# Expert slots of 256 rows, and half slots of 128 for an expert's remaining rows, in a conv-attention hybrid with a mixture of experts

## The chip, the core and the metric

The kernel runs on one core of one Trainium2 chip. The metric is the device time of one execution in microseconds (us); the time before is the median of three runs. The profile is one more execution, taken by the hardware profiler.

## What is computed

The input is an image of 256 channels and 64 x 64 places. A first layer does windowed linear attention on the normalized image and adds it. A second layer takes the 4096 places as tokens of 256 channels, adds a softmax attention of 8 heads, and then a mixture of experts, which is the part that the change touches:

```python
logits = xt @ Wr + br                       # 8 experts
top_p, top_idx = jax.lax.top_k(softmax(logits), 2)
weights = top_p / top_p.sum(axis=-1, keepdims=True)
xe = layernorm(xt) * ln_g + ln_b            # gain and shift of each expert
h = gelu(xe @ W1 + b1)                      # 256 -> 1024
y = h @ W2 + b2                             # 1024 -> 256
out = sum over the two chosen experts of weights * y
```

All of it is in f32. The reference works out every expert for every token; the kernel works out only the 2 x 4096 = 8192 pairs of token and chosen expert.

## The kernel before

The stages run one after the other: convolution and windowed attention, softmax attention, routing, expert slots, ending. The change touches routing and expert slots.

**Routing** (lines 1190 to 1365). The tokens' normalized rows z are made on ScalarE (L1224) in a buffer of their own and written to `zrows` in DRAM on SP's queue (L1228). VectorE finds each token's two experts and counts the rows of each expert (`upto`, L1271). A slot is 256 rows of one expert. Each expert gets as many slots as its rows fill, rounded up (`more`, `slots`, `ends`, L1276 to L1287). From `ends` come the expert of each slot (`past`, `owner`, `expert_of`, L1289 to L1297), a flag whether more than 36 slots are needed (`more_slots`, L1298), and the first row of each expert (`begins`). The place of each pair (`row`, then `at`, `pos`) is turned around by one-hot matmuls (L1334 to L1340: `line` and `piece` are built on VectorE and ScalarE for 8 token tiles at a time, and 64 bf16 matmuls add into one PSUM bank): for each row of each slot, the token to read (`source`) and the place to write (`target`). Rows that hold no token read token 0 and write to spare rows of `yrows`.

**Slots** (`run`, L1367 to L1432). The usual program has 36 slots; 3 more stand in a branch behind them, taken if `more_slots` is set (L1437 on). For each slot `weights` (L1170 to L1183) reads the slot's expert number into a register of SP and loads, on SP's queue and in this order, `cols` (first bias, gain and shift, L1179), `w1` (1 MB, L1180), `w2` (1 MB, L1181) and `b2` (L1182), each into one of two buffers. `load` also gathers two tiles of 128 rows from `zrows` with indirect DMAs on GpSimd (L1377; four buffers). `enter` transposes them on TensorE (L1391, four transposes) and applies gain and shift on VectorE (L1395). Then, for 8 hidden tiles, two matmuls add into a PSUM buffer `hp` of 256 columns (L1416; two buffers in turn), and ScalarE's Gelu empties it (L1417). After the first layer, `enter` of the next slot comes, and then the second layer: for each of the two row tiles 8 matmuls of 256 columns into `yp` (L1423), the bias added on VectorE (L1425), and an indirect DMA that scatters 128 rows to `yrows` (L1427). The framework's scheduler orders each engine's instructions by these dependences; so transposes and gathers can stand elsewhere than in the source.

**Ending** (L1442 on). Both experts' rows are read back, weighted, added to the tokens, transposed and written out.

Of the kernel before, what the change touches and what calls it, by code (L numbers as in the profile page):

```python
# [30 lines left out]
P = 128  # L31
# [15 lines left out]
NE = 8  # L47
HID = 1024
SLOT = 256
NS = (2 * N + NE * (SLOT - 1)) // SLOT  # L50
USUAL = 2 * N // SLOT + NE // 2
TAME = 60.0
# [8 lines left out]
    "k": {"sums": NCH // 4 * NW * D, "spread": NCH // 4 * NW * P, "before8": CH, "sides": NB * (SW + IMG + 1)},  # L61
    "m": {"rank": NE, "iota": P, "before": P, "ones": P, "number": 1, "high": 2 * NT, "spare": NS * SLOT // P},
}
# [7 lines left out]
def constants():  # L71
# [34 lines left out]
    out[:, _AT["high"]] = np.arange(2 * NT)[None, :]  # L106
    out[:, _AT["spare"]] = 1 + 2 * N + p[:, None] + P * np.arange(NS * SLOT // P)[None, :]
    return out
# [3 lines left out]
def tile_conv_attn_hybrid(ctx: ExitStack, tc: tile.TileContext, a: dict, out: bass.AP):  # L112
# [27 lines left out]
    def tok(i):  # L140
        return slice(P * i, P * (i + 1))
# [996 lines left out]


    with ExitStack() as phase:  # L1140
        pool = lambda name, bufs: phase.enter_context(tc.tile_pool(name=name, bufs=bufs))
# [6 lines left out]
        zrows = dram.tile([N, C], F32, name="zrows")  # L1148
        yrows = dram.tile([2 * N + NS * SLOT, C], F32, name="yrows")

# [11 lines left out]

        source = small.tile([P, NS * SLOT // P], mybir.dt.int32, name="source")
        target = small.tile([P, NS * SLOT // P], mybir.dt.int32, name="target")
        expert_of = small.tile([P, NS], mybir.dt.int32, name="expert_of")
        more_slots = small.tile([P, 1], mybir.dt.int32, name="more_slots")
# [3 lines left out]
        def weights(work, s):  # L1170

            e = nc.values_load(
                expert_of[:1, s : s + 1], engines=(mybir.EngineType.SP,), min_val=0, max_val=NE - 1
            )
            w1 = work.tile([P, KC, HID], F32, name="w1")
            w2 = work.tile([P, NH, C], F32, name="w2")
            b2 = work.tile([P, C], F32, name="b2")
            cols = work.tile([P, NH + 2 * KC], F32, name="cols")
            nc.sync.dma_start(cols, crows[bass.ds(e, 1)].rearrange("o p n -> p (o n)"))  # L1179
            nc.sync.dma_start(w1, a["L1_ffn_W1"][bass.ds(e, 1)].rearrange("o (k p) h -> p (o k) h", p=P))  # L1180
            nc.sync.dma_start(w2, a["L1_ffn_W2"][bass.ds(e, 1)].rearrange("o (k p) d -> p (o k) d", p=P))  # L1181
            nc.sync.dma_start(b2, a["L1_ffn_b2"][bass.ds(e, 1)].rearrange("o d -> (o d)").partition_broadcast(P))  # L1182
            return w1, w2, b2, cols  # L1183
# [6 lines left out]
        with ExitStack() as routing:  # L1190
            pool = lambda name, bufs: routing.enter_context(tc.tile_pool(name=name, bufs=bufs))
            r_ps = routing.enter_context(psum("r_ps", 2))
            bank, _ = banks(r_ps)
            big = pool("r_big", 1)
            r_work = pool("r_work", 2)
# [25 lines left out]
            nc.vector.scalar_tensor_tensor(less, norm.mean, -1.0, again, op0=ALU.mult, op1=ALU.mult)  # L1221
            z = big.tile([P, NT, C], F32, name="z")
            for i in range(NT):
# [21 lines left out]
            for n in range(2):  # L1245
# [26 lines left out]


            iota = cst["iota"]
            steps = small.tile([P, N // SLOT], F32, name="steps")
            nc.vector.tensor_scalar_mul(steps, iota[:, : N // SLOT], float(SLOT))  # L1276
            more = small.tile([P, NE, N // SLOT], F32, name="more")
            nc.vector.tensor_tensor(
                more,
                upto[:, :, NT - 1].unsqueeze(2).to_broadcast([P, NE, N // SLOT]),  # L1280
                steps.unsqueeze(1).to_broadcast([P, NE, N // SLOT]),
                ALU.is_gt,
            )
            slots = small.tile([P, NE], F32, name="slots")
            nc.vector.tensor_reduce(slots, more, AX.X, ALU.add)
            ends = small.tile([P, NE], F32, name="ends")
            nc.vector.tensor_tensor_scan(ends, on[:, 0, 1 : NE + 1], slots, 0.0, op0=ALU.mult, op1=ALU.add)  # L1287
            past = small.tile([P, NS, NE], F32, name="past")
            nc.vector.tensor_tensor(  # L1289
                past,  # L1290
                iota[:, :NS].unsqueeze(2).to_broadcast([P, NS, NE]),
                ends.unsqueeze(1).to_broadcast([P, NS, NE]),
                ALU.is_ge,
            )
            owner = small.tile([P, NS], F32, name="owner")
            nc.vector.tensor_reduce(owner, past, AX.X, ALU.add)
            nc.vector.tensor_scalar_min(expert_of, owner, NE - 1.0)  # L1297
            nc.vector.tensor_single_scalar(more_slots, ends[:, NE - 1 :], float(USUAL), op=ALU.is_gt)  # L1298
            begins = small.tile([P, NE], F32, name="begins")
            nc.vector.tensor_sub(begins, ends, slots)  # L1300
            nc.vector.tensor_scalar_mul(begins, begins, float(SLOT))

            row = small.tile([P, NE, NT], F32, name="row")
            nc.vector.tensor_sub(row, upto, per_tile)
            nc.vector.tensor_add(flat(row), counts[:, : NE * NT], flat(row))
            nc.vector.tensor_add(row, row, begins.unsqueeze(2).to_broadcast([P, NE, NT]))

# [3 lines left out]

            NPC = NS * SLOT // P
            G = 8
# [3 lines left out]
            for n in range(2):  # L1317
# [13 lines left out]
                for i8 in range(0, NT, G):  # L1331
                    some = lambda v, n: v[:, i8 : i8 + G].unsqueeze(1).to_broadcast([P, n, G])
                    line = r_work.tile([P, P, G], BF16, name="line")
                    nc.vector.tensor_tensor(line, some(within, P), counter, ALU.is_equal)  # L1334
                    piece = r_work.tile([P, 3, NPC, G], BF16, name="piece")
# [3 lines left out]
                    for i in range(G):  # L1339
                        nc.tensor.matmul(  # L1340
                            back[:, : 2 * NPC].rearrange("p (m n) -> p m n", m=2),
                            line[:, :, i],
                            piece[:, 1:, :, i],
                            start=n == 0 and i8 + i == 0,
                            stop=n == 1 and i8 + i == NT - 1,
                        )

            for n in range(2):
# [18 lines left out]
        def run(slots, work, ps):  # L1367


            def load(s):  # L1370

                of = weights(work, s)
                xs = []
                for j in range(SLOT // P):
                    xs.append(work.tile([P, C], F32, name="xs", bufs=4))
                    q = SLOT // P * s + j
                    nc.gpsimd.indirect_dma_start(  # L1377
                        out=xs[j],
                        out_offset=None,
                        in_=zrows[:, :],  # L1380
                        in_offset=bass.IndirectOffsetOnAxis(ap=source[:, q : q + 1], axis=0),
                    )
                return *of, xs

            def enter(slot):

                *_, cols, xs = slot
                tp = ps.tile([P, KC, SLOT], F32, tag="tp", name="ps_tp")
                for j in range(SLOT // P):
                    for k in range(KC):  # L1390
                        nc.tensor.transpose(tp[:, k, tok(j)], xs[j][:, tok(k)], ident)  # L1391
                xe = work.tile([P, KC, SLOT], F32, name="xe")
                for k in range(KC):
                    gain, shift = (slice(NH + KC * n + k, NH + KC * n + k + 1) for n in range(2))
                    nc.vector.tensor_scalar(  # L1395
                        xe[:, k, :],
                        tp[:, k, :],
                        cols[:, gain],
# [7 lines left out]
            xe = enter(ahead)  # L1406
            for s in slots:
                slot, x_now = ahead, xe
                if s + 1 in slots:
                    ahead = load(s + 1)  # L1410
                w1, w2, b2, cols, _ = slot
                hid = work.tile([P, NH, SLOT], F32, name="hid")
                for n in range(NH):
                    hp = ps.tile([P, SLOT], F32, tag="hp", name="ps_hp")
                    for k in range(KC):
                        nc.tensor.matmul(hp, w1[:, k, tok(n)], x_now[:, k, :], start=k == 0, stop=k == KC - 1)  # L1416
                    nc.scalar.activation(hid[:, n, :], hp, AF.Gelu, bias=cols[:, n : n + 1])  # L1417
                if s + 1 in slots:
                    xe = enter(ahead)
                for j in range(SLOT // P):  # L1420
                    yp = ps.tile([P, C], F32, tag="yp", name="ps_yp")
                    for n in range(NH):
                        nc.tensor.matmul(yp, hid[:, n, tok(j)], w2[:, n, :], start=n == 0, stop=n == NH - 1)  # L1423
                    y = work.tile([P, C], F32, name="y", bufs=4)
                    nc.vector.tensor_add(y, yp, b2)  # L1425
                    q = SLOT // P * s + j
                    nc.gpsimd.indirect_dma_start(  # L1427
# [5 lines left out]

        run(range(USUAL), slot_work, experts.enter_context(psum("m_ps", 2)))
        experts.close()
        more_slots = nc.values_load(more_slots[:1, :1], min_val=0, max_val=1)  # L1436
        with (  # L1437
# [3 lines left out]
        ):  # L1441
            run(range(USUAL, NS), work, ps)  # L1442

# [58 lines left out]
```

## Time and profile before

| what | us |
|---|---|
| median of 3 runs (2933.38 to 2937.23) | 2935.82 |
| the profiled execution | 2937.02 |
| its span, first to last instruction | 2935.2 |

| stretch, us from the span's start | stage | length | PE busy | DVE busy | ACT busy | GB/s |
|---|---|---|---|---|---|---|
| 0 to 1060 | convolution, windowed attention | 1060.0 | 989.25 | 760.88 | 334.86 | |
| 1060 to 2310 | softmax attention | 1250.0 | 1240.48 | 1192.27 | 1022.79 | 5 |
| 2310 to 2374 | routing | 64.0 | 32.21 | 38.82 | 27.39 | 153 |
| 2374 to 2889.5 | 36 expert slots | 515.5 | 515.29 | 65.18 | 136.36 | 183 |
| 2889.5 to 2935.2 | ending | 45.7 | 17.45 | 26.04 | 11.57 | 279 |

How to read it: PE is TensorE's matmuls, PEld its weight loads, DVE is VectorE, ACT is ScalarE, POOL is GpSimd, SP issues DMAs. In a timeline line stand the start, the length, the engine, the line of the kernel, the operation, tile written <- tiles read, the shapes and how many were merged, and in brackets the idle time before and what ended it. In a line of groups stand, behind the count, the busy time in us and the mean in ns of one, then the idle time before. A TensorE operation in f32 shows as two records for each matmul and one for each transpose, each with its own weight load.

### The profile page before, as it was taken

The numbers are of one execution on the slowest core, as the hardware profiler recorded it, in microseconds if no ns is written. First come the engines' busy times: TensorE is split into PE (matmuls) and PEld (weight loads), VectorE is DVE, ScalarE is ACT, GpSimd is POOL, SyncE is SP. The second block draws the span as 40 slices with busy tenths as digits, with TensorE's granted clock in tenths as the row PEclk, the third lists the DMA queues.
The fourth block names the chain that finished last, engine by engine and source line by source line (L and its number), as shares of the span: only waits on it lengthen the run. The fifth ranks groups of instructions, "written<-read, shape, count | busy, mean of one in ns | idle before, by whom it ended". The sixth has DMA issues, their size and how long they took to land. (4 is left out here: it accounts for less than half of the span.)

```text
span 2935.2 us, 63107 instructions
## 1 busy us (share of the span) xinstructions
PE 2794.7 (95%) x26358; PEld 1352.3 (46%) x26358; DVE 2083.2 (71%) x3005; ACT 1533.0 (52%) x2134; POOL 720.3 (25%) x816
## 2 busy tenths in 40 slices
PE   6899999989999989999999999999999699999996
PEld 5466442735644354222222222222222268888884
DVE  5776768577677877999999999999999821111113
ACT  3242323124233213888888888888888622222222
POOL 1085858119485621000000000000000022222220
PEclk9999999999999999999999999999999879999997
DMA  5000000000000000000000000000000155555555
GB/s 142 6 3 3 2 3 2 7 1 3 4 2 3 1 19 1 5 5 5 5 5 5 5 5 5 5 5 5 5 5 5 53 182 200 191 189 195 192 196 198
DMA packets 97930, 137.35 MB, mean 47 GB/s; under 512 B 18242, under 2 KB 79272, under 8 KB 97636
## 3 DMA queue, kind: packets, MB, share of 16 engines
q1 hardware_dynamic: 82360, 105.31, 10.9%
q0 software_dynamic: 6912, 18.88, 2.2%
q10 hardware_dynamic: 8364, 9.02, 0.9%
q8 instruction: 210, 3.44, 0.5%
q14 instruction: 84, 0.69, 0.1%
HBM read 115.07 MB, written 18.12 MB: 45 GB/s over the span
## 5 line engine op out<-in xcount | busy, mean ns | idle before, releaser
L1001 ACT ACTIVATE pe<-ps_two 128x1024 f32<-128x1024 f32 x1024 | 993.1, 1022 | 150.0 <-PE ps_two L991 145.4
L1008 DVE TENSOR_TENSOR total<-total,pe 128x1024 f32<-128x1024 f32 x928 | 1058.2, 1217 | 0.0
L991 PE MATMUL ps_two<-qk 32*128 32x512 f32 x4096 | 629.1, 639 | 3.6 <-POOLq L946 1.9
L959 PE MATMUL ps_acc<-pe,v 128*32 128x512 f32 x4096 | 546.4, 605 | 0.1
L554 ACT COPY sm<-ps_sc 128x384 f32<-128x384 f32 (+4 forms) x486 | 232.4, 512 | 459.5 <-PE ps_sc L678 276.4
L558 POOL TENSOR_TENSOR sm<-sm,mask 128x192 f32<-128x192 f32 (+3 forms) x460 | 380.2, 861 | 231.6 <-ACT sm L554 231.0
L991 PEld LDWEIGHTS ps_two<-qk 32*128 32x128 f32 x4096 | 204.8, 183 | 418.7 <-PE ps_two L991 222.2
L558 DVE TENSOR_TENSOR sm<-ps_sc,mask 128x384 f32<-128x384 f32 (+3 forms) x708 | 324.2, 518 | 91.7 <-PE ps_sc L678 90.2
L1417 ACT ACTIVATE hid<-ps_hp,cols 128x256 f32<-128x256 f32 x288 | 136.4, 473 | 382.8 <-PE ps_hp L1416 382.0
L1266 POOL MEMSET on<- 128x256 f32 x1 | 0.3, 311 | 1175.1 <-PE ps_den L959 1175.1
L959 PEld LDWEIGHTS ps_acc<-pe,v 128*32 128x32 f32 x4096 | 80.7, 108 | 389.4 <-issue 376.2
L1416 PE MATMUL ps_hp<-xe,w 128*128 128x256 f32 x1152 | 257.0, 381 | 0.0
L1423 PE MATMUL ps_yp<-w,hid 128*128 128x256 f32 x1152 | 254.6, 379 | 0.0
L678 PE MATMUL ps_sc<-qk 32*128 32x192 f32 (+3 forms) x2688 | 245.3, 446 | 5.2 <-DVE sm L558 2.9
L1423 PEld LDWEIGHTS ps_yp<-w,hid 128*128 128x128 f32 x1152 | 216.4, 190 | 28.1
L1416 PEld LDWEIGHTS ps_hp<-xe,w 128*128 128x128 f32 x1152 | 208.5, 190 | 42.1 <-ACT hid L1417 5.0
L694 PE MATMUL ps_acc<-sm,v 128*32 128x192 f32 (+3 forms) x2688 | 216.6, 423 | 0.8 <-POOL sm L558 0.8
L1395 DVE TENSOR_SCALAR xe<-ps_tp,cols 128x256 f32<-128x256 f32 x72 | 35.9, 540 | 248.8 <-PE ps_tp L1391 228.7
L558 POOL TENSOR_TENSOR sm<-sm,ycut 128x384 f32<-128x384 f32 (+4 forms) x150 | 150.7, 1025 | 140.4 <-ACT sm L554 140.2
L678 PEld LDWEIGHTS ps_sc<-qk 32*128 32x128 f32 x2688 | 126.4, 186 | 124.0 <-DVE sm L558 70.4
L1425 DVE TENSOR_TENSOR y<-ps_yp,b 128x256 f32<-128x256 f32 x72 | 30.6, 425 | 208.1 <-PE ps_yp L1423 208.1
L558 DVE TENSOR_TENSOR sm<-ps_sc,ycut 128x512 f32<-128x512 f32 (+4 forms) x250 | 127.7, 562 | 64.8 <-PE ps_sc L609 62.7
(231 smaller groups left out, 2252.5 us busy)
## 6 DMA issues: line engine op xcount, KB each, us to landing
w<-in_L_ffn_W SPq DMA_DIRECT2D x72, 1024.0 KB
b<-in_L_ffn_b SPq DMA_DIRECT2D x36, 128.0 KB
rows<-in_x SPq DMA_DIRECT2D x16, 256.0 KB
zrows<-z SPq DMA_DIRECT2D x4, 1024.0 KB
y<-yrows SPq DMA_DIRECT2D x8, 512.0 KB
y<-yrows ACTq DMA_DIRECT2D x8, 512.0 KB
rec<-recs SPq DMA_DIRECT2D x60, 64.0 KB
x<-in_x ACTq DMA_DIRECT2D x4, 512.0 KB
```

The source lines that it names most:

```text
L554: nc.scalar.copy(sm[:, :used], sc[:, :used])
L558: engine.tensor_mul(to, of, mk.unsqueeze(1).to_broadcast(list(to.shape)))
L678: nc.tensor.matmul(scs[h][:, at : at + n], kT[hs[h], tok(i)], qT[hs[h], CH * ix + CELL * c0 : CH * ix + CELL * c1], start=True, stop=True, ...
L694: nc.tensor.matmul(acc[hs[h], CELL * c0 : CELL * c1], v[:, i, hs[h]], sms[h][:, at : at + n], start=not begun[0], stop=last and at == plac ...
L959: nc.tensor.matmul(to[D * hd : D * (hd + 1), :], lhsT(hd), rhs[:, hd, :], start=start, stop=stop, skip_group_check=True,)
L991: nc.tensor.matmul(sc[hd // 2][:, hd % 2, :], qk[hs, 1, g, tok(i)], qk[hs, 0, g, chunk(qc)], start=True, stop=True,)
L1001: nc.scalar.activation(pe[:, pair, :], s, AF.Exp, scale=C**-0.5)
L1008: add = nc.vector.tensor_add(to, first[:, pair, :] if i == 1 else to, pe[:, pair, :])
L1395: nc.vector.tensor_scalar(xe[:, k, :], tp[:, k, :], cols[:, gain], cols[:, shift], op0=ALU.mult, op1=ALU.add,)
L1416: nc.tensor.matmul(hp, w1[:, k, tok(n)], x_now[:, k, :], start=k == 0, stop=k == KC - 1)
L1417: nc.scalar.activation(hid[:, n, :], hp, AF.Gelu, bias=cols[:, n : n + 1])
L1423: nc.tensor.matmul(yp, hid[:, n, tok(j)], w2[:, n, :], start=n == 0, stop=n == NH - 1)
```

## The change

A row block of 128 becomes the unit. An expert gets one whole slot of 256 rows for each 256 of its rows, and one more if over 128 are left; if 1 to 128 are left, it gets a half slot of 128 rows. The whole slots stand first (32 of them, 64 units), the half slots behind (up to 8). The usual program has 32 whole slots and 4 half ones, a half one after whole slots 4, 12, 20 and 28 (counted from 0); 4 more units of 128 rows, each with its own load of weights, stand in the branch. `more_slots` is set if more than 68 units are needed.

In a half slot the first layer's matmuls and Gelus have 128 columns instead of 256, and the second layer has one row tile. The weights are loaded whole for each slot as before. `w1` and `w2` get three buffers each, `cols` and `b2` keep two. z is put into the attention's activation buffer `act`. `begins` has a second half for the half slots, and `row` gets it where a row lies behind its expert's whole slots (`rest`, `inside`). The experts of the slots (`owners`) are worked out later, after the second `line` of the one-hot matmuls. The one-hot pieces get 72 instead of 78 columns.

```diff
-NS = (2 * N + NE * (SLOT - 1)) // SLOT
-USUAL = 2 * N // SLOT + NE // 2
+NS = 2 * N // SLOT
+NU = 2 * NS + NE
+USUAL = 2 * NS + NE // 2
...
-            w1 = work.tile([P, KC, HID], F32, name="w1")
-            w2 = work.tile([P, NH, C], F32, name="w2")
+            w1 = work.tile([P, KC, HID], F32, name="w1", bufs=3)
+            w2 = work.tile([P, NH, C], F32, name="w2", bufs=3)
...
-            z = big.tile([P, NT, C], F32, name="z")
+            z = act.rearrange("p k n -> p (k n)").rearrange("p (i c) -> p i c", c=C)
...
-            nc.vector.tensor_scalar_mul(steps, iota[:, : N // SLOT], float(SLOT))
+            nc.vector.tensor_scalar(
+                steps, iota[:, : N // SLOT], float(SLOT), float(P), op0=ALU.mult, op1=ALU.add
+            )
...
+            size = small.tile([P, 2, NE], F32, name="size")
+            nc.vector.tensor_reduce(size[:, 0], more, AX.X, ALU.add)
+            inside = small.tile([P, NE], F32, name="inside")
+            nc.vector.tensor_scalar_mul(inside, size[:, 0], float(SLOT))
+            nc.vector.tensor_tensor(size[:, 1], total, inside, ALU.is_gt)
+            nc.vector.tensor_scalar_mul(size[:, 0], size[:, 0], 2.0)
...
+            def owners():
...
+                nc.vector.tensor_reduce(owner, past, AX.X, ALU.add)
+                nc.vector.tensor_copy(expert_of, owner)
+                nc.vector.tensor_single_scalar(expert_of, expert_of, NE - 1, op=ALU.bitwise_and)
+                nc.vector.tensor_single_scalar(more_slots, ends[:, 1, NE - 1 :], float(USUAL), op=ALU.is_gt)
...
-            nc.vector.tensor_add(row, row, begins.unsqueeze(2).to_broadcast([P, NE, NT]))
+            by_tile = lambda v: v.unsqueeze(2).to_broadcast([P, NE, NT])
+            rest = small.tile([P, NE, NT], F32, name="rest")
+            nc.vector.tensor_tensor(rest, row, by_tile(inside), ALU.is_ge)
+            nc.vector.tensor_mul(rest, rest, by_tile(begins[:, 1]))
+            nc.vector.tensor_add(row, row, by_tile(begins[:, 0]))
+            nc.vector.tensor_add(row, row, rest)
...
+                    if n == 0 and i8 == G:
+                        with tc.issue_after(made.ins):
+                            owners()
...
-                        nc.tensor.matmul(hp, w1[:, k, tok(n)], x_now[:, k, :], start=k == 0, stop=k == KC - 1)
-                    nc.scalar.activation(hid[:, n, :], hp, AF.Gelu, bias=cols[:, n : n + 1])
+                        nc.tensor.matmul(
+                            hp[:, :n], w1[:, k, tok(m)], x_now[:, k, :n], start=k == 0, stop=k == KC - 1
+                        )
+                    nc.scalar.activation(hid[:, m, :n], hp[:, :n], AF.Gelu, bias=cols[:, m : m + 1])
...
-        run(range(USUAL), slot_work, experts.enter_context(psum("m_ps", 2)))
+        usual = []
+        for s in range(NS):
+            usual.append((2 * s, 2 * s + 1))
+            if s % (2 * NS // NE) == NS // NE:
+                usual.append((2 * NS + s // (2 * NS // NE),))
+        assert len(usual) == NS + USUAL - 2 * NS
+        run(usual, slot_work, experts.enter_context(psum("m_ps", 2)))
...
-            run(range(USUAL, NS), work, ps)
+            run([(q,) for q in range(USUAL, NU)], work, ps)
```

## The prediction

> **What bounds the kernel now.** I read the page first (busy shares by slice), then busy time by stage, then the timeline of one slot, then the groups split by shape, for durations of the shapes that the change makes more of.
>
> Page, the slices, and two groups:
>
> ```profile
> PE   6899999989999989999999999999999699999996
> PEclk9999999999999999999999999999999879999997
> L1416 PE MATMUL ps_hp<-xe,w 128*128 128x256 f32 x1152 | 257.0, 381 | 0.0
> L1423 PE MATMUL ps_yp<-w,hid 128*128 128x256 f32 x1152 | 254.6, 379 | 0.0
> ```
>
> The expert slots are the last stretch of 9s, with the clock granted nearly in full. Between 2374.0 and 2889.5 us TensorE is busy 515.29 of 515.50 us: it sets the time there, and 36 slots run in it (1152 records over 32 a slot). One slot on the timeline:
>
> ```profile
> 2618.44 7.09 PE L1416 MATMUL ps_hp<-xe,w 128*128 128x256 f32 x32
> 2619.55 0.47 ACT L1417 ACTIVATE hid<-ps_hp,cols 128x256 f32<-128x256 f32 x1 [7.79 <-PE ps_hp L1416]
> 2620.08 5.05 PEld L1416 LDWEIGHTS ps_hp<-xe,w 128*128 128x128 f32 x24 [0.15 <-ACT hid L1417]
> ...
> 2625.36 0.60 PE L1391 MATMUL ps_tp<-cst,xs 128*128 128x128 f32 x4
> ...
> 2625.80 7.07 PE L1423 MATMUL ps_yp<-w,hid 128*128 128x256 f32 x32
> ...
> 2632.71 0.59 PE L1416 MATMUL ps_hp<-xe,w 128*128 128x256 f32 x2
> ```
>
> From start to start: first layer 2625.36 - 2618.44 = 6.92 us (32 records, 0.216 each), four transposes 0.44 (0.11 each), second layer 6.91, in all 14.27 us. A matmul in f32 is two records. ScalarE is idle 0.39 to 0.41 us between Gelus, so it follows TensorE. The line at 2620.08 is the one to keep: the third group of a slot reuses the first group's PSUM buffer (there are two), and its weight load starts 0.06 after that Gelu ends (2619.55 + 0.47). Here this is just in time.
>
> **What the change does to the slots.** The eight experts' row counts, worked out by the reference on its own inputs, are 1063, 1010, 1041, 992, 1033, 995, 1042, 1016. Before: 5+4+5+4+5+4+5+4 = 36 slots, all in the usual program. After: the remainders over 1024 are 39, 17, 9 and 18, so four half slots, and the others still fill four whole ones: 32 whole and 4 half, 68 units, exactly the usual program. The extra branch stays untaken (68 is not above 68). So four slots of 14.27 us become half slots.
>
> Cost of a half slot on TensorE. The second layer has one row tile of 8 matmuls instead of two: 16 records x 0.216 = 3.46. It has two transposes: 0.22. The first layer keeps its 16 matmuls and their weight loads, with 128 moving columns instead of 256: 32 records. Two things can keep these from costing half.
>
> First the weight load that goes with each record. The nearest row is an f32 matmul of 128 columns with its own 128x128 weights in the convolution stage:
>
> ```profile
> 591.83 0.30 PEld L436 LDWEIGHTS ps_two<-cstk,kt 128*128 128x128 f32 x2
> 591.89 0.43 PE L436 MATMUL ps_two<-cstk,kt 128*128 128x128 f32 x2
> 592.05 0.30 PEld L440 LDWEIGHTS ps_two<-cstk,kt 128*128 128x128 f32 x2
> 592.16 0.34 PE L440 MATMUL ps_two<-cstk,kt 128*128 128x73 f32 x2
> 592.27 0.19 PEld L355 LDWEIGHTS ps_two<-act,w 128*128 128x128 f32 x1
> ```
>
> Loads start 0.22 apart for two, so 0.11 each, while the matmuls run; the transposes above (each with its own load) also take 0.11. The Trainium skill, "TensorE: Matmul & The Clock Gate", section "The mechanism", speaks against the change: weight loads overlap a running matmul only where the row groups differ; its section "LDWEIGHTS (loading the stationary operand)" gives a load as columns over 1.2, 107 ns for 128. By that rule a record would be 0.107 + 0.107 = 0.214, the first layer would cost as much as a whole one (6.85), a half slot 0.22 + 6.85 + 3.46 = 10.53, and the change only 4 x 3.74 = 15.0 us. By the rows the load hides and the record is 0.11 (at worst 0.135, the 0.27 from L436's start to L440's over two): first layer 3.52 (4.32). I take the rows; L1416's own 0.216 leaves no room for a load in series either, as twice 0.11 is all it has.
>
> Second, ScalarE. A group of two matmuls lasts 4 x 0.11 = 0.44 and its Gelu of 128 columns is not in the trace. Bounds from the copies of the same engine out of PSUM:
>
> ```profile
> L554 ACT COPY sm<-ps_sc 128x384 f32<-128x384 f32 x250 | 110.5, 482 | 187.3 <-PE ps_sc L678 146.8 <-PE ps_sc L609 32.6 <-POOL sm L558 7.6
> L554 ACT COPY sm<-ps_sc 128x256 f32<-128x256 f32 x24 | 8.2, 374 | 24.2 <-PE ps_sc L609 24.2
> ```
>
> (482 - 374)/128 = 0.84 ns a column, so 473 - 108 = 365 ns; the floor is half of 473, 237. With two PSUM buffers, groups go in pairs. Pair begins at 0: first group's last record starts at 0.33, lasts about 0.27 (L1391's mean is 290), Gelu starts some 0.06 later, 0.66, ends at 1.03; weight load 0.06 later, matmul 0.11 after that: 1.20. The pair needs 0.88 of TensorE, so it waits. The built order puts the next slot's four transposes one after each pair, which fills 0.11 of each gap. First layer with these four transposes: 3 x 1.20 + 0.88 + 0.11 = 4.59 instead of 3.52 + 0.44 = 3.96. Half slot, without the next slot's transposes: 0.22 + 4.15 + 3.46 = 7.83 (bounds: 7.20 if the wait is all covered, 8.2 with a Gelu of still 473 ns, whose pair takes 1.31). Each saves 14.27 - 7.83 = 6.44, four 25.8 us.
>
> **What else moves in the slots.** Weights are still loaded whole, 36 times, so four loads come 7.8 us after the one before instead of 14.3. The windows show the ceiling:
>
> ```profile
> 2500.00:2700.00 200.00, 200.00 (x955) 171.41 (x954) 25.83 (x56) 53.02 (x112) 55.00 (x56) 1.00 0.59 194
> 2615.00:2617.00 2.00, 2.00 (x11) 1.77 (x10) 0.42 (x1) 0.00 (x0) 1.00 (x1) 1.00 1.02 418
> ```
>
> Last two columns: DMA share and GB/s. The mean is 194, the burst while one weight matrix comes in 418. In the built order SP's queue takes, for slot s+1, cols (waits for the last Gelu of slot s-1), w1 and w2 (with a third buffer no wait beyond that), b2 (waits for the last y of slot s-1; the loads of s+2 are queued behind it). The slot after a half one thus has its weights issued after the first layer of the slot before the half: 6.91 + 7.83 = 14.7 us ahead, against about 2.1 MB: the three windows of 2 us from 2619 (120, 371 and 173 GB/s, one matrix and the gathers) carried 1.3 MB in 6 us, so 10 us. Hidden; the third buffer is what lets w2 go out with w1, since before it was issued only after the slot's last matmul (2618.63). The gathers (L1377), one for a half slot as its one scatter, stand one to two slots ahead of their transposes in POOL's order and y and xs keep four buffers: no wait that I can find; price 0, and a few us if one is late.
>
> **Routing, before the first slot (2310 to 2374).** On VectorE from "more" (2337.84) to "at" (2340.70) there are 2.86 us now. The four operations on the slots' owners leave this path (0.48, 0.47, 0.18 and 0.15 busy, but overlapping: some 0.9 from start to start); three more of 128x256 (0.42 busy, about 0.41 apart) and four more of at most 16 columns (0.16 busy, about 0.17 apart) come in, 1.9. Net +1.0. The owners' past and reduce over 640 elements (0.48 for 312, so about 0.8 each) with four small ones, some 2.2 us, fall in VectorE's wait of 2.84 us before 2349.20; if that cover were gone, up to 2.2. The expert numbers come 9 us later, about 2349.5; SP's queue has the weight loads behind them, w1 goes out near 2352 instead of 2343, and the first L1416 starts at 2373.85, so 20 us hide it; what they no longer collide with is the zrows writes. z in act's place waits for the last L940, ended 2321.6, while z starts at 2330. The one-hot matmuls, 64 of 156 columns at 0.283 in series, get 144: between nothing and 64 x 0.022 = 1.4 gained; I take 0.7, as no row separates load from stream there. Net +0.3 (from -0.4 to +3).
>
> **Sum.** -25.8 + 0.3 = -25.5 us. The profiled execution took 2937.02 (span 2935.2), 1.2 above the median of 2935.82, so 2911.5 for it and 2910.3 for the median.
>
> **Rivals.**
> - Half is half: Gelu and handshakes fit under a pair's matmuls and transpose (0.99). For it: ScalarE is idle 0.39 of each 0.87. Against: 1.20, and still 1.07 with a Gelu of 237. Half slot 7.20: -28.3 + 0.3, 2907.8.
> - Weight loads in series, the skill's rule: -15.0 + 0.3, 2921.1. Against: L436 and L1391.
> - A load or gather is late at each half slot, up to 3 us: 2911 to 2922. Against: 14.7 us of lead.
> - Loads cannot go above their mean of 194 GB/s: 36 loads then take the time of 36 slots, no gain, 2936. Against: 418.
> - The slower side: the branch is taken. Place: after the usual slots. If routing on the chip gave 69 units or more, four half slots follow, each with its own load of 2.1 MB: about 10 for the first load and gather, then 4 x 8 with nothing else to hide behind, +42: 2935.8 - 25.5 + 42 = 2952. It decides at one unit, for which some expert must cross a multiple of 128 upwards: the nearest is 1016, 9 rows short. In the reference's scores only 4 tokens have second and third expert within 0.001. So 3 in 100.
>
> **Chances.** Likeliest case 0.66 (2908 to 2914), half is half 0.14, series 0.06, late transfers 0.08, no gain 0.03, branch 0.03. The range 2905 to 2918 takes in the first two and the better part of late transfers. About 0.2% (6 us) is what a measurement of this kernel can tell: faster by more 0.94, within it 0.03, slower 0.03.
>
> **What would show it.** In the profile after: L1416's counterpart in two shapes, 1024 records of 256 columns and 128 of 128; L1417 256 of 256 columns and 32 of 128 at 365 ns; a half slot of 7.8 us, the weight loads of its pairs waiting for ACT, three waits of 0.2 to 0.3 each. A half slot near 10.5 with no ACT wait is the series rival; a pause at the start of L1416 or L1423 of the slot after a half one is the late load; L1416 in a second program past the usual slots is the branch. I am wrong if whole slots are no longer 14.27.

## The result, and the profile after

| | before | after |
|---|---|---|
| median, us (5 runs each) | 2935.91 | 2909.11 |
| lowest to highest | 2933.38 to 2937.83 | 2907.35 to 2911.62 |
| profiled execution, us | 2937.02 | 2911.62 |
| its span | 2935.2 | 2909.8 |

The ratio is 0.9907, 95% interval 0.9893 to 0.992: 26.8 us less, where 25.5 were forecast. The two profiled executions differ by 25.4. Runs of one kernel differ by up to 4.5, so the medians alone cannot tell the 26.8 from the 25.5; the stretches of the traces below are finer.

On the page of the changed kernel the slots' slices look as they did, nine tenths busy at a clock granted nearly in full (a slice is a fortieth of the span, so counting slices does not show the saving):

```profile
PE   6899999989999988999999999999999969999996
PEclk9999999999999999999999999999999969999997
```

The groups split by shape, in the stretch of the slots (count, busy us, mean ns, idle before):

```profile
L1453 PE MATMUL ps_hp<-xe,w 128*128 128x256 f32 x1024 | 228.5, 381 | 0.0
...
L1456 ACT ACTIVATE hid<-ps_hp,cols 128x256 f32<-128x256 f32 x256 | 121.4, 474 | 326.3 <-PE ps_hp L1453 326.3
...
L1453 PE MATMUL ps_hp<-xe,w 128*128 128x128 f32 x128 | 18.1, 284 | 0.0
...
L1456 ACT ACTIVATE hid<-ps_hp,cols 128x128 f32<-128x128 f32 x32 | 11.8, 368 | 34.1 <-PE ps_hp L1453 33.0
```

There are 1024 first-layer records of 256 columns and 128 of 128, so 32 whole and 4 half slots, and none behind them: the branch was not taken. A Gelu of 128 columns takes 368 ns. The first half slot on the timeline:

```profile
2448.05 1.05 PE L1453 MATMUL ps_hp<-xe,w 128*128 128x128 f32 x8
...
2448.74 0.77 ACT L1456 ACTIVATE hid<-ps_hp,cols 128x128 f32<-128x128 f32 x2 [7.15 <-PE ps_hp L1453]
...
2448.94 0.27 PE L1428 MATMUL ps_tp<-cst,xs 128*128 128x128 f32 x1
2449.16 0.97 PEld L1453 LDWEIGHTS ps_hp<-xe,w 128*128 128x128 f32 x8 [0.19 <-ACT hid L1456]
2449.16 1.16 PE L1453 MATMUL ps_hp<-xe,w 128*128 128x128 f32 x8
...
2450.33 1.16 PE L1453 MATMUL ps_hp<-xe,w 128*128 128x128 f32 x8
...
2451.50 1.16 PE L1453 MATMUL ps_hp<-xe,w 128*128 128x128 f32 x8
...
2452.60 3.62 PE L1462 MATMUL ps_yp<-w,hid 128*128 128x256 f32 x16
```

Eight records are a pair of groups; inside a pair the records start 0.111 to 0.112 apart. After the first pair comes one transpose of the next slot, and the next pair's weight load waits for the Gelu. The second to fourth pair start 1.17 us apart (2449.16, 2450.33, 2451.50), the first 1.11 before the second, though each holds only 0.89 of matmuls and 0.11 of transpose. From start to start the half slot lasts 8.01 us with the next slot's four transposes in it, and so do the other three; the slot before it, with two transposes instead of four, lasts 14.05. A half slot's own share is thus 8.01 - 0.22 = 7.79, and it saves 14.27 - 7.79 = 6.48.

Where the time went, by starts of instructions in the two traces. `chosen` (the sum of the two one-hot choices on VectorE, at 2333.80 before and 2335.68 after) stands ahead of everything that the change alters but z's buffer; the 1.88 us between the two is within the spread of earlier stages (2332.96 to 2337.86 in all the profiles here).

| stretch | before | after | difference |
|---|---|---|---|
| chosen to first first-layer matmul | 40.05 | 39.56 | -0.49 |
| first slot's start to last slot's start | 501.44 | 475.51 | -25.93 |
| last slot's start to the end | 59.95 | 59.09 | -0.86 |

The second row is four times 6.48 (25.92); the first slot is 0.31 shorter, and one whole slot took 14.55, as its first Gelu came 0.28 later than in other slots and TensorE waited for it (why it came later stays open). The third row is within the spread of the ending: another profile of the kernel before, with z changed only (below), has 59.20. The sum is -27.28; with the 1.88 by which the changed kernel came later to `chosen` it is the profiles' -25.4.

### The profile page after: what moved, and what is told of

Its sections match the earlier page's. It is cut to its first block, busy times and chain, and to the rows that moved or that the text cites. A ratio compares the mean times of both kernels' runs of the same rounds, so it can differ in the third digit from the quotient of the medians.

```text
span 2909.8 us, 62928 instructions
## 1 busy us (share of the span) xinstructions
PE 2769.2 (95%) x26286; PEld 1329.9 (46%) x26286; DVE 2082.3 (72%) x3009; ACT 1529.6 (53%) x2134; POOL 712.4 (24%) x808
## 5 line engine op out<-in xcount | busy, mean ns | idle before, releaser
L1456 ACT ACTIVATE hid<-ps_hp,cols 128x256 f32<-128x256 f32 (+1 forms) x288 | 133.1, 462 | 360.4 <-PE ps_hp L1453 359.3
L1453 PE MATMUL ps_hp<-xe,w 128*128 128x256 f32 (+1 forms) x1152 | 246.6, 370 | 0.0
L1462 PE MATMUL ps_yp<-w,hid 128*128 128x256 f32 x1088 | 240.8, 379 | 0.0
L1453 PEld LDWEIGHTS ps_hp<-xe,w 128*128 128x128 f32 x1152 | 201.1, 190 | 39.7 <-ACT hid L1456 5.6
L1462 PEld LDWEIGHTS ps_yp<-w,hid 128*128 128x128 f32 x1088 | 204.2, 190 | 26.4
L1432 DVE TENSOR_SCALAR xe<-ps_tp,cols 128x256 f32<-128x256 f32 (+1 forms) x72 | 34.8, 525 | 239.3 <-PE ps_tp L1428 217.5
L561 POOL TENSOR_TENSOR sm<-sm,ycut 128x384 f32<-128x384 f32 (+4 forms) x150 | 150.8, 1024 | 140.9 <-ACT sm L557 140.6
```

The costliest lines, as they stand in the source:

```text
L561: engine.tensor_mul(to, of, mk.unsqueeze(1).to_broadcast(list(to.shape)))
L1432: nc.vector.tensor_scalar(xe[:, k, :n], tp[:, k, :n], cols[:, gain], cols[:, shift], op0=ALU.mult, op1=ALU.add,)
L1453: nc.tensor.matmul(hp[:, :n], w1[:, k, tok(m)], x_now[:, k, :n], start=k == 0, stop=k == KC - 1)
L1456: nc.scalar.activation(hid[:, m, :n], hp[:, :n], AF.Gelu, bias=cols[:, m : m + 1])
L1462: nc.tensor.matmul(yp, hid[:, m, tok(j)], w2[:, m, :], start=m == 0, stop=m == NH - 1)
```

## Experiments

The ratios below are against runs of the kernel before on the same chip.

**Four PSUM buffers for the first layer.**

```diff
-                    hp = ps.tile([P, SLOT], F32, tag="hp", name="ps_hp")
+                    hp = ps.tile([P, SLOT], F32, tag="hp", name="ps_hp", bufs=4)
```

> The changed kernel with four instead of two PSUM buffers for the first layer's groups (hp). Theory (a half slot costs 0.6 us more than half because its groups of 0.44 us go in pairs that wait 1.17 us for the Gelu of 0.37 and its handshakes): with four buffers the wait goes, the half slot with the next slot's transposes falls from 8.01 to about 7.4 us, four half slots save 2.4 us, and whole slots stay at 14.27. Rival (the weight loads, 0.11 each at best, set the pace in the half slot too): 8.01 stays, no change. Rival (ScalarE's own Gelus are the bound, 0.37 each): 8 x 0.40 = 3.2 us are less than the matmuls' 3.5, so no.

Measured: 2906.40 us, ratio 0.9892 (0.9875 to 0.9908); its interval overlaps the change's, so what follows rests on the trace. Its half slots take 7.46 us, its whole ones 14.25. The timeline of its first half slot:

```profile
2446.13 3.73 PE L1453 MATMUL ps_hp<-xe,w 128*128 128x128 f32 x32
...
2446.82 3.44 ACT L1456 ACTIVATE hid<-ps_hp,cols 128x128 f32<-128x128 f32 x8 [7.15 <-PE ps_hp L1453]
...
2449.70 0.60 PE L1428 MATMUL ps_tp<-cst,xs 128*128 128x128 f32 x4
...
2450.14 3.62 PE L1462 MATMUL ps_yp<-w,hid 128*128 128x256 f32 x16
```

All 32 records run through in 3.57 us, 0.112 each, each with its own weight load; the wait for the Gelu is gone (between 2440 and 2850 us the weight loads of the first layer wait 5.0 us for Gelus in the changed kernel, and in this one such a wait is no longer listed). So the 0.55 us by which a half slot was longer than its matmuls was that wait, and the loads do not set the pace. The saving of four half slots is 2.2 us; from the first slot's start to the last one's it is 3.9, mainly as the first slot also falls, from 16.85 to 15.01.

**Two buffers for w1 and w2.**

```diff
-            w1 = work.tile([P, KC, HID], F32, name="w1", bufs=3)
-            w2 = work.tile([P, NH, C], F32, name="w2", bufs=3)
+            w1 = work.tile([P, KC, HID], F32, name="w1")
+            w2 = work.tile([P, NH, C], F32, name="w2")
```

> The changed kernel with two buffers for w1 and w2 as before, instead of three. Theory (the loads have 14 us or more ahead of their use with either count; the third buffer is not what hides them): slots stay at 14.27 and 8.01 us, time within 1 us of the changed kernel's. Rival (the prediction's sentence that the third buffer is what lets w2 go out with w1, and that this hides the load behind a short slot): the slot after a half one starts its second layer late, some 1 to 3 us at each of four places, 4 to 12 us slower than the changed kernel.

Measured: 2911.16 us, ratio 0.9906 (0.989 to 0.9923). Slots of 14.27 and 8.01 as in the changed kernel, from first to last 475.34 us against 475.51. With two buffers the second weight matrix for the slot behind the first half slot is issued 6.05 us after the first (2443.66 and 2449.71), with three 0.61 after it (2442.20 and 2442.81), and no matmul waits for a weight in either. The third buffer brings nothing here: the rival, which is the prediction's own sentence, falls. In the routing it even seems to cost: from `chosen` to the first slot it is 38.88 us with two buffers and 39.56 with three, most of it before the first gather (see the end).

**The owners in their old place.** `owners()` is called ahead of `row`, and no longer inside the one-hot loop.

> The changed kernel with the slots' owners worked out where they were before, ahead of row, instead of in VectorE's wait during the one-hot matmuls. Theory (before the change ScalarE's z held up the first one-hot piece by 1.0 us, the change's longer chain on VectorE used this up and both now arrive together): the four owner operations, about 2.2 us, now come on the path; from the last counting scan to the first one-hot matmul about 1.5 to 2.2 us more than in the changed kernel, the time up by that, less than what the rounds can tell. Rival (still hidden behind z): no change in this stretch.

Measured: 2913.50 us, ratio 0.9919 (0.9902 to 0.9935), which is not told apart from the change. In the trace `at` starts 1.37 us later, the first one-hot matmul 1.54, the first slot 1.48 (41.04 against 39.56 after chosen). Of 1.37 us more on VectorE, 1.54 and 1.48 arrive: in the changed kernel there is no cover left for more work there.

**The half slots in a row.**

```diff
-            if s % (2 * NS // NE) == NS // NE:
-                usual.append((2 * NS + s // (2 * NS // NE),))
+            if s == NS // NE:
+                usual += [(q,) for q in range(2 * NS, USUAL)]
```

> The changed kernel with its four half slots in a row after whole slot 4, instead of spread. The same work. Theory (weights are hidden while they have time: a load of 2.1 MB every 7.8 us is 273 GB/s, with gathers and scatters some 300, against bursts of 370 to 418): near the limit, the loads of the third and fourth half slot and of the slot behind come late, some 2 to 8 us in all, seen as a wait at the start of a first or second layer; spread half slots show none. Rival (the ceiling is well above): 8.01 us each, no change. Rival (the mean of 194 GB/s is a ceiling): each of them takes 11 to 12 us, 12 to 16 us more.

Measured: 2910.99 us, ratio 0.9904 (0.9888 to 0.9921). The four take 30.87 us, 7.72 each, with no wait for a load. That is less than 8.01, as three of the four hold two transposes instead of four, and the scheduler put two records of the second layer where the fourth pair waits for its buffer. The rival was right: no load comes late. With a DMA share of 0.92, though, the DMA engines were nearly always at work. The window over them (last two columns DMA share and GB/s):

```profile
2448.00:2486.00 38.00, 38.00 (x236) 33.68 (x236) 5.30 (x13) 14.61 (x38) 9.82 (x10) 1.00 0.92 305
```

**The same with two buffers for w1 and w2.**

> The four half slots in a row after whole slot 4, with two buffers for w1 and w2 instead of three. Theory (the third buffer's use is to have a load more ahead where half slots follow each other): here, unlike with spread half slots, it matters, and each half slot of the row waits 1 to 3 us for a load, 3 to 10 us in all. Rival (a load at 330 GB/s is fast enough with two): 7.7 us each as with three.

One profiled execution: the four again take 30.87 us, from first to last slot 475.31, at 298 GB/s. The third buffer does not matter here either, though this rests on one execution; my second reading of its use fell as well.

**Half slots only.**

```diff
-            usual.append((2 * s, 2 * s + 1))
+            usual += [(2 * s,), (2 * s + 1,)]
```

> The changed kernel with every whole slot run as two half slots: 68 half slots, each with its own load of weights, the same rows. Theory (four half slots in a row took 7.7 us each with the DMA engines about fully busy at some 330 GB/s, 2.5 MB a slot, so matmuls and loads need the same time): half slots of 7.7 to 8.5 us throughout, 68 of them 525 to 575 us instead of 490, the kernel 2945 to 2995 us, slower than before the change; weight loads of TensorE or first matmuls wait for DMA w. Rival (the four in a row lived on what three buffers had fetched ahead, and sustained the loads give 200 GB/s, the mean of the profile before): 12 us each, 3150 us.

Measured: 2963.44 us, ratio 1.0083 (1.0065 to 1.0101), slower than the kernel before. Three windows of its slots:

```profile
2500.00:2600.00 100.00, 99.06 (x629) 87.19 (x627) 14.18 (x39) 36.24 (x99) 25.95 (x27) 1.00 0.96 315
2600.00:2700.00 100.00, 98.98 (x619) 86.32 (x619) 12.79 (x36) 36.83 (x102) 24.07 (x25) 1.00 0.95 311
2700.00:2800.00 100.00, 99.01 (x613) 86.34 (x612) 12.75 (x36) 35.61 (x97) 23.57 (x24) 1.00 0.94 306
```

TensorE is still busy 99 of 100 us while the loads run at 306 to 315 GB/s. In the list of waits from 2450 to 2850 us, TensorE's largest is 25.6 us of first-layer weight loads waiting for Gelus, and no matmul waits for a weight DMA. Most half slots take 7.62 or 8.12 us. So the loads are hidden even when each comes with half a slot's work, and the rival of 200 GB/s is out. The expected time came, but not for the expected reason: the waits for w that were to go with it are not there. As a half slot takes more than half of 14.27, 68 of them cost more than the work of 34 whole slots in the changed kernel, and more than the 36 of the kernel before; that four hp buffers would give all of it back was not tried.

**The branch taken.** `USUAL` is one unit less and the last half slot is left out of the usual program, so that the branch runs five units.

> The changed kernel with three half slots in the usual program instead of four, so that the 68th unit needs the branch, which runs five units of 128 rows (one with rows, four spare). The prediction's price of a taken branch, for five units: one half slot less in the usual program, -8; about 10 for the first load and gather, then 5 x 8: +42, 2951 us. Rival (the branch's first load is hidden behind the usual program's end): +32. Rival (entering it costs more, each engine waiting for all others and code being fetched): above +50.

Measured: 2959.37 us, ratio 1.0068 (1.0048 to 1.0088). The seam on the timeline:

```profile
2848.32 7.07 PE L1462 MATMUL ps_yp<-w,hid 128*128 128x256 f32 x32
...
2856.13 0.97 POOL L1465 DMA_INDIRECT yrows<-y,target  x1 [2.48 <-DVE y L1464]
2859.09 0.34 SPq L1184 DMA_DIRECT2D cols<-crows  x1
2859.38 0.99 POOL L1413 DMA_INDIRECT xs<-zrows,source  x1 [2.28 <-DMA yrows<-y,target]
...
2866.63 0.66 PE L1428 MATMUL ps_tp<-cst,xs 128*128 128x128 f32 x2 [11.24 <-DMA xs<-zrows,source]
...
2872.82 3.45 PE L1453 MATMUL ps_hp<-xe,w 128*128 128x128 f32 x16
```

Between the end of the usual program's last matmul (2855.2) and the branch's first (2872.82) TensorE has only a few transposes for 17.6 us: no load or gather of the branch is issued before the last scatter is. Then the weights of two slots and four gathers are issued between 2859.1 and 2863.3, and from 2864 to 2873 the DMA engines are busy at a share of 0.99 and carry 249 GB/s. The first gather is issued at 2859.38 and first read at 2866.63. The clock granted from 2860 to 2873 is 0.50. The five half slots then take 39.8, the first of them 8.53. With one half slot less in the usual program that is +49.6 (17.6 + 39.8 - 7.8), and 2.4 come back in the ending.

**Three hp buffers, and two for w1 and w2.**

> The changed kernel with three hp buffers instead of two, and with two buffers for w1 and w2 instead of three. Theory (a buffer is free 1.17 us after its group starts; three groups of a half slot last 1.34 us): three buffers are enough, a half slot with the next slot's transposes takes 7.46 us as with four, whole slots 14.25; and w1 and w2 need two buffers only. About 2906 us. Rival (four were needed): half slots between 7.46 and 8.01. Rival (third w buffer needed once half slots are this short): waits behind the half slots.

Measured: 2907.02 us, ratio 0.9885 (0.9867 to 0.9903). Half slots of 7.46, whole ones of 14.25: behind the first slots three buffers are as good as four, as the 1.17 us of a buffer's round trip and 3 x 0.45 of matmuls say (the first slot takes 15.72 here and 15.01 with four). From first to last slot it takes 472.06 us against the change's 475.51. The intervals of the ratios overlap; by the stretches of the trace it is the better version, and it needs 16 KB less for each partition (a third buffer for two matrices of 1 MB over 128 partitions).

**A quarter of z on GpSimd**, in the kernel before and in the changed one.

```diff
             for i in range(NT):
...
+                if i % 4 == 3:
+                    nc.gpsimd.tensor_scalar(
+                        z[:, i, :], t[:, i, :C], again[:, i : i + 1], less[:, i : i + 1], op0=ALU.mult, op1=ALU.add
+                    )
...
```

> The kernel before, with every fourth tile of z made on GpSimd instead of ScalarE. Theory (in the kernel before, ScalarE's z ends 1.0 us after VectorE's first one-hot piece is ready, and holds up the copy of that piece and with it the one-hot matmuls): z's end on ScalarE comes some 4 us earlier and the first one-hot matmul about 1.0 us earlier, at 11.9 instead of 12.95 us after chosen. Rival (VectorE's chain was the limit, as the prediction had it): still 12.95.

> The changed kernel with every fourth tile of z made on GpSimd. Theory (here VectorE's chain is 1.0 us longer and ends together with z): the first one-hot matmul stays at 12.9 us after chosen, within 0.1. Rival (ScalarE still is the limit): earlier by up to 1 us.

One profiled execution each. ScalarE in the kernel before, then in it with z shared:

```profile
2340.49 5.51 ACT L1224 ACTIVATE z<-t,less,rstd 128x256 f32<-128x256 f32 x11
2345.90 1.51 ACT L1337 ACTIVATE piece<-piece,cstm 128x624 bf16<-128x624 bf16 x2
```

```profile
2340.89 2.06 ACT L1229 ACTIVATE z<-t,less,rstd 128x256 f32<-128x256 f32 x4
...
2346.91 1.52 ACT L1342 ACTIVATE piece<-piece,cstm 128x624 bf16<-128x624 bf16 x2 [2.31 <-DVE piece L1341]
```

In the kernel before, the copy of the first one-hot piece starts the moment z is done; with z shared, it waits for VectorE instead. From `at` to the first one-hot matmul it is 6.06 us before and 5.06 with z shared; in the changed kernel 5.02, and 4.99 with z shared. Counted from chosen, as the expectations count, it is 12.95 and 12.20 in the kernel before, and 12.91 and 13.12 in the changed one: both miss the expected 11.9 and 12.9 by some 0.2 to 0.3, as VectorE reached `at` 0.24 later in both with GpSimd at work beside it (why was not tested). In the changed kernel with z shared the one-hot matmuls took 2.5 us longer; there the scheduler put part of the owners behind the third line. The first slot came 2.1 us later.

## Why the prediction was right

The mechanism and its size held, in the slots point by point:

- 68 units and an untaken branch: the record counts say so.
- The record of 128 columns: 0.11 forecast, 0.111 to 0.112 measured, with its own weight load. The rule of the Trainium skill that was weighed against it ("TensorE: Matmul & The Clock Gate", "The mechanism": loads overlap only where row groups differ) would have made it 0.214. The same section also names a background weight buffer as a second case in which a load is pulled ahead, which the prediction left out. Here loads and matmuls of the same 128 rows overlap (32 records in 3.57 us); the rows L436 and L1391 of the trace before were the ones to go by.
- The Gelu: 365 ns forecast, 368 measured. The pair: 1.20 forecast, 1.17 measured for two of the three intervals and 1.11 for the first. With four buffers the wait went, as the theory asked; a half slot then is 7.46 - 0.22 = 7.24, close to the 7.20 of the rival that half is half. So with two buffers that rival is out, and the wait is what separates the two.
- A half slot: 7.83 forecast, 7.79 measured. Four of them: 25.8 against 25.92.
- The loads: hidden. The sentence that the third buffer is what lets w2 go out ahead was true of the issue, but what it suggests, that this hides the load, was not: two buffers do, even for half slots in a row.

The term that was wrong is the routing: +0.3 forecast, -0.49 measured. The end of VectorE's chain, the copies of the first piece on ScalarE and the first one-hot matmul stand so in the kernel before and in the changed one:

```profile
2340.70 1.12 DVE L1319 TENSOR_TENSOR at<-hot,row 128x256 f32<-128x256 f32 x2
...
2345.90 1.51 ACT L1337 ACTIVATE piece<-piece,cstm 128x624 bf16<-128x624 bf16 x2
...
2346.76 3.54 PE L1340 MATMUL ps_acc<-piece,line 128*128 128x156 bf16 x12 [10.21 <-ACT piece L1337]
```

```profile
2343.57 1.12 DVE L1352 TENSOR_TENSOR at<-hot,row 128x256 f32<-128x256 f32 x2
...
2347.26 0.82 DVE L1369 TENSOR_TENSOR piece<-which,counter 128x576 bf16<-128x576 bf16 x2
2347.77 1.43 ACT L1370 ACTIVATE piece<-piece,cstm 128x576 bf16<-128x576 bf16 x2
...
2348.59 1.74 PE L1373 MATMUL ps_acc<-piece,line 128*128 128x144 bf16 x6 [10.17 <-ACT piece L1370]
```

"Net +1.0" for VectorE's chain was exact (2.86 from `more` to `at` before, 3.86 after), but that 1.0 us was not on the path. It was put there because VectorE was busy through that stretch; the end of the stretch is the first copy of a piece on ScalarE, and in the kernel before that copy stood behind z, as the run with z shared shows. The cover was 1.0 us, and the change used all of it. In sum:

| term of the routing | forecast | measured |
|---|---|---|
| VectorE's chain, `more` to `at` | +1.0 | +1.00 |
| `at` to the first one-hot matmul (6.06 to 5.02), the cover | 0 | -1.04 |
| one-hot matmuls, first start to last (17.72 to 16.77) | -0.7 | -0.95 |
| last write of `target` to the first gather (0.37 to 0.94, by starts) | 0 | +0.57 |
| the rest | 0 | -0.07 |
| sum | +0.3 | -0.49 |

The one-hot matmuls' starts are 0.266 apart instead of 0.281. That the routing's sum came within 0.8 of its forecast is in part luck: an overlooked cover and an unforeseen delay of the gather have opposite signs.

The price of the slower rival was a little low: for five units 42 were expected and the ratios put it at some 47 above the change (0.0161 of 2940). The gap at the seam, 17.6 instead of 10, less the 2.4 of the ending, is the missing part: there the loads of two slots and the gathers are issued together, and the clock is at 0.50. How the 17.6 divides among these was not tested.

## What to carry to other kernels

Before counting on half the work for half the columns, work out the round trip of the buffer between two engines: here it was 1.17 us for two groups of 0.45, and in the traces a third PSUM buffer was worth 3.3 us (475.34 to 472.06 from first to last slot), a third copy of the weights nothing. Price a longer chain on one engine only after asking which engine's instruction ends that stretch: its queue may hold unrelated work that covers the chain. Loading the same weights once more was free here, as the transfers fitted beside the shorter work; whether they will is read from bursts in short windows, not from a mean that only shows the demand.

## What the runs showed that I had not expected

- The DMA engines carried 306 to 315 GB/s over 300 us while TensorE stayed 99% busy; their share was 0.94 to 0.96. The mean of 194 before was demand.
- The first gather of the changed kernel is issued 0.94 us after the start of the last write of its index and target, in all versions with three buffers for w1 and w2 and z on ScalarE alone; with two buffers it is 0.37, as before. In the trace the gather waits for 11 semaphores in the one case and for 5 in the other; with three buffers and z shared it waits for 9 and comes after 0.36. So the count alone is not the cause, and it stays open.
- In the half-slot program, TensorE's order mattered: where the scheduler put transposes and two second-layer records between pairs, a half slot took 7.62 us; where it put nothing between them, 8.12, with the same buffers and two transposes in both.
